# Layer 1's values by seven products, as a fourth stream beside queries, keys and outputs

## The chip, the cores and the metric

One Trainium2 chip, one core of it. The metric is device time in microseconds (us) of one execution. All data is 32-bit floating point. Engines: PE (TensorE, matmuls; its weight loads are listed as PEld), DVE (VectorE), ACT (ScalarE), POOL (GpSimd), SP (SyncE, which issues the transfers here).

## The reference

An image of 128 rows of 256 positions with 256 channels passes through two attention layers, each with a group normalization ahead of it and the input added behind it. Layer 0 is full attention inside each row (8 heads of 32) with a softmax, an added bias and a gate. Layer 1, where the change is, is attention inside each row too, in 4 heads of 64, where a position sees only positions at most 16 away:

```
qkv = x2 @ w_in.T + b_in                 # x2: 128 rows x (256 positions, 256 channels)
q, k, v = split(qkv)
scores = q k^T / 8, kept where |i - j| <= 16
out = softmax(scores) v
y = out @ w_out.T + b_out                # then x + y
```

## The kernel before, in words

Layer 1 handles two rows (a pair, number `i`) at a time; 64 pairs, of which the main loop runs over 63 (`i` = 0 to 62). A pair's normalized input `1xn` is [128 channels, 4, 256 positions], the 4 being (row, channel half).

A projection of a pair is a product of a 2x2 block weight with a 2x2 block input (two channel halves by two rows). The scheme used, with seven block products in place of eight (class `Seven`; `Summed` in layer 1), needs four sums of weight quarters (`Quarters`, made once, during layer 0) and four sums of input quarters (`1ts`, `row_sums`, on POOL: one 128x512 and two 128x256 subtractions). A stream's product `n` is written to one half of a PSUM bank; some products accumulate onto what is there, after ACT or DVE has taken the previous sum (`take`, L685 to L708). `in_turn` issues the streams in lockstep: product 2 of every stream, then product 1 of every stream, and so on in the order 2, 1, 5, 6, 7, 4, 3. While one stream's sum is taken, PE works for the others. There are three streams: `q` and `k` of pair `i + 1` and the output projection `o` of pair `i - 2`.

The values `v` of a pair do not go that way. `values` (L1380) computes them plainly, per row: 16 matmuls of 128x64 tokens with 128 output channels, eight block products in all. The result is stored by tokens: partition = position within a block of 64, with one half of the partitions for heads 0 and 1 (`half` 0) and the other for heads 2 and 3. One ACT copy per row (L1389) takes it.

One turn of the main loop issues, in this order (the order is written out by hand for all five engines, `manual_schedule`; nothing is reordered):

- `scores` of the two rows of pair `i` (L1409), ACT's exponentials (L1417), POOL's mask product `1p` (L1419) and sum `1zp` (L1426);
- `finish(i - 3)`: DVE transposes (L1562) and four stores of 128 KB (L1572) on SP's queue;
- `attend(i - 1)`: weights times values into `1av` (L1450; two PSUM banks, of which there is only one set, `bufs=1`), sums of weights `1zs` (L1462);
- `sums` (L1473, L1474) and three partial reciprocals `1rz` on DVE (`inverse`, L1487), the first at once, the other two inside the stretch after products 1 and 5;
- `stretch(i + 1, i - 2)`: the 21 products of the three streams, with `by_transfer(i - 1)` after product 5: `1rz` is written to `rz_far` (L1495, two small transfers) and read back, spread over partitions, as `1near` (L1499, two of 256 KB), on SP's queue;
- `normal(i + 2)`: the next input load `yg` (L796, 512 KB, SP's queue), four ACT activations into `1xn` (L1333), POOL's `1ts`;
- `divide(i - 1)`: two DVE products `1at` = `1av` x `1near` (L1519), which free `1av` for the next `attend`; then POOL's `row_sums` into `1att`;
- `bounds(i - 1)` (a DVE reduction L1528 and an ACT pass L1530 for a later check);
- `values` of the two rows of pair `i + 1`.

PSUM: `1av` and `1zs` have their own banks; scores, streams and values rotate through four banks of one ring (`proj_bank`).

Of the kernel before, what the change touches and what calls it, by code (L numbers as in the profile page):

```python
# [15 lines left out]
P = 128  # L16
# [23 lines left out]
def conv_preact_kernel(  # L40
# [536 lines left out]
    def row_sums(t, x, engine):  # L577

        engine.tensor_tensor(t[:, 0::2], x[:, 2:4], x[:, 0::2], ALU.subtract)  # L579
        engine.tensor_tensor(t[:, 1], x[:, 3], t[:, 0], ALU.subtract)  # L580
        engine.tensor_tensor(t[:, 3], x[:, 1], t[:, 1], ALU.subtract)
# [151 lines left out]
                    next(amid, lambda: None)()  # L733
                yield

    def in_turn(sevens, amid=lambda n: None, between=iter(())):


        for p in sevens:
            p.open()  # L740

            p.product(2, p.ps[:, 1, :], first=True)
            p.take(2)
        next(between, None)
        for n in (1, 5, 6, 7, 4, 3):
            for p in sevens:
                p.product(n)
                p.take(n)
            if n in (1, 5):
                amid(n)  # L750
            next(between, None)
        for _ in between:
            pass

    def one_by_one(w, at, name, done, width):

# [19 lines left out]
    with ExitStack() as both:  # L776
# [1 line left out]

        stats1 = st1.tile([P, 2, S // 2 + 2, 6], F32, name="stats1")
        most1 = Most(st1, stats1, 4, 1)  # L780
        quarters1 = {w: Quarters(st1, w_in_t, n * C, f"1{w}") for n, w in enumerate("qk")}
        quarters1["o"] = Quarters(st1, w_out_t, 0, "1o")
        ygs, pools = {}, {}
        rz_far = dram.tile([2, 2, 4, R], F32, name="rz_far")
# [3 lines left out]
        def load1(g):  # L788
            if g * XG < S and g not in ygs:

                if g % 7 < 2:
                    yg = big.tile([P, XG * (R // B), C // A], F32, tag="xg", name=f"yg{g}")
                    yg = yg.rearrange("p n c -> p (n c)").rearrange("p (s h q) -> p s h q", h=2, q=R)
                else:
                    yg = pools["yg"].tile([P, XG, 2, R], F32, tag="yg", name=f"yg{g}", bufs=5)
                nc.sync.dma_start(out=yg, in_=rows(x1, g * XG, XG))  # L796
                ygs[g] = yg
# [493 lines left out]
        with ExitStack() as lay:  # L1291
# [27 lines left out]

            shift1 = att.tile([P, 2], F32, name="shift1", bufs=1)  # L1320

            def normal(i, by_scalar):

                if 2 * i >= S:
                    return
                load1(i + 1)
                xns[i] = row.tile([P, 4, R], F32, tag="xn", name=f"1xn{i}", bufs=2)
                for r in range(2):
                    for half in (1, 0):
                        x, y = xns[i][:, 2 * r + half, :], ygs[i][:, r, half, :]  # L1330
                        col = slice(half, half + 1)
                        if by_scalar:
                            nc.scalar.activation(x, y, AF.Identity, bias=shift1[:, col], scale=rstd1[:, col])  # L1333
                        else:
                            nc.vector.tensor_scalar(
                                x, y, mean1[:, col], rstd1[:, col], op0=ALU.subtract, op1=ALU.mult
                            )
                tss[i] = row.tile([P, 4, R], F32, tag="ts", name=f"1ts{i}", bufs=2)
                row_sums(tss[i], xns[i], nc.gpsimd)

            def project(s):

# [18 lines left out]
                    st[2 * i + r].update({w: p.to[:, 2 * r : 2 * r + 2, :] for w, p in zip("qk", streams)})  # L1361
                return streams

            def stretch(i, j, amid=lambda n: None, between=iter(())):

                streams = projections(i)
                if j >= 0:
                    outputs[j] = Summed(row, quarters1["o"], ats[j], ats_t[j], f"1o{j}", "out", bias=bo_v, y=ygs[j])
                    streams.append(outputs[j])
                in_turn(streams, amid, between)  # L1370

            def values(s):
                if s >= S:
                    return
                i, r = divmod(s, 2)
                ps = proj_bank(f"p1v{s}").rearrange("p a (b c) -> p (a b) c", c=P)
                for b in range(NB):
                    for kt in range(2):
                        for half in range(2):
                            nc.tensor.matmul(  # L1380
                                ps[KB * half : KB * (half + 1), b, :],
                                lhsT=xns[i][:, 2 * r + kt, KB * b : KB * (b + 1)],
                                rhs=w_in_t[:, kt, 2 * C + P * half : 2 * C + P * (half + 1)],
                                start=(kt == 0), stop=(kt == 1),
                            )
                    if b < NB - 1:
                        yield
                v = row.tile([P, NB, P], F32, tag="v", name=f"1v{s}")
                nc.scalar.copy(v, ps)  # L1389
                st[s]["v"] = v  # L1390
                yield

            def all_values(rows):

                for s in rows:
                    yield from values(s)

            def scores(s, engine=nc.gpsimd):
                q, k = st[s]["q"], st[s]["k"]
# [29 lines left out]
            def attend(i):  # L1429

                if i < 0:
                    return

                if i < S // 2 - 1:
                    av = ps_av.tile([P, 2, 2, R], F32, tag="av", name=f"1av{i}", bufs=1)
                    av = [av[:, half] for half in range(2)]
                else:
                    av = [proj_bank(f"1av{i}_{half}") for half in range(2)]
                zs = ps_av.tile([P, 2, 2, R], F32, tag="zs", name=f"1zs{i}", bufs=1)
                zps = []  # L1440
                for r in range(2):
                    (p, zp), v = hd.pop(2 * i + r), st[2 * i + r]["v"]
                    zps.append(zp)
                    for b in range(NB):
                        for half in range(2):
                            for j in range(2):
                                keys, cols = slice(KB * half, KB * (half + 1)), slice(D1 * j, D1 * (j + 1))
                                q0, p0 = QLO[b], R * (b % 2) + QLO[b]

                                nc.tensor.matmul(  # L1450
                                    av[half][cols, r, q0 + QIN[b].start : q0 + QIN[b].stop],
                                    lhsT=v[keys, b, cols],
                                    rhs=p[keys, j, p0 + QIN[b].start : p0 + QIN[b].stop],
                                    start=(r == 0 and b == 0), stop=(b == NB - 1),
                                    skip_group_check=True,
                                )

                for r in range(2):
                    for half in range(2):
                        for j in range(2):  # L1460
                            keys = slice(KB * half, KB * (half + 1))
                            nc.tensor.matmul(  # L1462
                                zs[strip(2 * j + r), half, 0, :], lhsT=place[keys, :], rhs=zps[r][keys, j, :],
                                start=True, stop=True,
                            )
                hd["av", i] = (av, zs)
# [119 lines left out]
            with tc.manual_schedule(engines={  # L1586
# [9 lines left out]
                for i in range(last):  # L1596
                    s = 2 * i
                    scores(s)
                    scores(s + 1)
                    if i == 0:  # L1600
                        for _ in all_values(range(2)):
                            pass
                        normal(i + 2, True)
                        for _ in all_values(range(2, 4)):
                            pass
                        continue
                    finish(i - 3)
                    attend(i - 1)
                    sums(i - 1)
                    inverse(i - 1, 0)  # L1610

                    def amid(n):
                        inverse(i - 1, 1 if n == 1 else 2)
                        if n == 5:
                            by_transfer(i - 1)

                    stretch(i + 1, i - 2, amid, all_values(range(s + 2, s + 4)) if i == 1 else iter(()))
                    normal(i + 2, True)
                    divide(i - 1)
                    if 0 <= i - 1 < last - 2:  # L1620
                        ats_t[i - 1] = row.tile([P, 4, R], F32, tag="att", name=f"1att{i - 1}", bufs=2)
                        row_sums(ats_t[i - 1], ats[i - 1], nc.gpsimd)
                    bounds(i - 1)
                    if i > 1:
                        for _ in all_values(range(s + 2, s + 4)):
                            pass

                def all_of(s):
                    for _ in project(s):
# [6 lines left out]
                        store(s)  # L1636

                scores(S - 2)
                finish(last - 3)
                scores(S - 1, nc.vector)  # L1640
                attend(last - 1)
# [229 lines left out]
```

## Time and profile before

| | |
|---|---|
| time, median of 3 runs | 3087.22 us (3086.99 to 3087.53) |
| profiled execution: its time, its span | 3088.84 us, 3086.7 us |
| mean granted PE clock | 0.993 |
| from 2100 to 2300 us (layer 1): PE busy | 199.12 of 200 us |
| same stretch: PEld, DVE, ACT, POOL busy | 150.82, 131.57, 108.36, 139.44 us |
| same stretch: share of the DMA engines, rate | 0.43, 101 GB/s |
| layer 1: first product to end of the span | 2025.5 to 3086.7 us |

The span is what the profiler saw between the first and the last instruction; the execution's own time is 2.1 us longer. "Busy" is the time in which an engine had an instruction running; a matmul's row overlaps the next one's, so a duration in its row is longer than the distance between two starts. The chain of work that ended last lists pieces in the order in which each released the next; for PE its pieces are distances, and can be summed. "Idle before" with a releaser tells what an engine waited for. Offsets in the text are in us.

### The profile page before, as it was taken

To read this page: it belongs to the slowest core of one execution; us is meant where nothing else is said; L and a number is where in the kernel's file an instruction comes from. 1 tells how busy PE (TensorE), PEld (TensorE's weight loads), DVE (VectorE), ACT (ScalarE), POOL (GpSimd) and SP (SyncE) were. 2 spreads that over 40 slices of the span, in tenths; PEclk is the share of its full clock that TensorE was granted. 3 is DMA by queue.
4 is the path that set the end of the run, shared out by engine and by line. 5 is a ranking of instruction groups with operands and counts; after the bars stand their busy time and mean duration, and the time that the engine had idled before them with its cause. 6 is when DMAs were issued, how large, how long until landed. Compare 5 with 4: busy or idle time off the path is not lost.

```text
span 3086.7 us, 142499 instructions
## 1 busy us (share of the span) xinstructions
PE 3004.4 (97%) x62701; PEld 2062.4 (67%) x62701; DVE 2248.5 (73%) x4503; ACT 1913.6 (62%) x4327; POOL 1901.1 (62%) x1913
## 2 busy tenths in 40 slices
PE   7779999999999999999999999999999999999997
PEld 4546666666666666666666666677777777777775
DVE  4667787878787877787788778756666666666665
ACT  4656666667666766676667666655555555555553
POOL 3035666656665666566656565566677777777674
PEclk9989999999999999999999999999999999999999
DMA  9941222222222221222222222124444444444443
GB/s 379 424 135 45 62 65 62 50 64 65 62 50 63 65 61 49 65 64 60 52 65 62 61 52 65 58 64 102 102 96 100 105 99 99 97 104 99 98 98 71
DMA packets 385413, 280.84 MB, mean 91 GB/s; under 512 B 285104, under 2 KB 354192, under 8 KB 378640
## 3 DMA queue, kind: packets, MB, share of 16 engines
q1 hardware_dynamic: 383888, 269.27, 33.0%
q8 instruction: 494, 8.09, 1.1%
q0 software_dynamic: 752, 2.36, 0.2%
q14 instruction: 135, 1.11, 0.1%
q10 hardware_dynamic: 144, 0.00, 0.0%
HBM read 202.38 MB, written 69.17 MB: 88 GB/s over the span
## 4 chain that ended last, share of the span: by engine, by line
PE 91%; DMA 5%; DVE 2%; POOL 1%; issue 0%; ACT 0%; SPq 0%; DVEq 0%; POOLq 0%; ACTq 0%
PE sim L840 9%; PE av L872 7%; PE p1v L1380 7%; PE p1q L587 6%; PE pbv L936 6%; PE po L587 6%; PE p1k L587 6%; PE p1o L587 6%; PE pq L587 6%; PE pv L587 6%; PE pk L587 5%; PE pg L587 5%; PE zs L885 4%; PE 1sim L1409 3%; DMA pr<-in_L_conv_pair_repr_dram 3%; PE 1av L1450 3%
## 5 line engine op out<-in xcount | busy, mean ns | idle before, releaser
L853 ACT ACTIVATE ex<-sim 128x512 f32<-128x512 f32 x1024 | 555.2, 606 | 253.3 <-PE sim L840 253.3
L862 DVE TENSOR_TENSOR both<-ex 128x512 f32<-128x512 f32 x508 | 445.5, 896 | 65.7 <-ACT ex L853 65.4
L631 POOL TENSOR_TENSOR v<-v,midv 128x512 f32<-128x512 f32 x64 | 82.1, 1283 | 453.9 <-ACT v L625 453.9
L840 PE MATMUL sim<-q,k 32*64 32x256 f32 x8192 | 289.3, 388 | 1.3 <-ACT ex L853 1.3
L965 DVE RECIPROCAL rz<-zs 128x256 f32<-128x256 f32 x128 | 224.9, 1757 | 67.8 <-PE zs L885 55.9
L872 PE MATMUL av<-ex,v 128*32 128x256 f32 x4096 | 244.7, 379 | 1.6 <-DVE at L1030 1.6
L1419 POOL TENSOR_TENSOR 1p<-1ex,seen 128x768 f32<-128x768 f32 x127 | 231.4, 1822 | 11.4 <-ACT 1ex L1417 11.4
L691 ACT ACTIVATE 1q<-p1q,bqk 128x256 f32<-128x256 f32 x192 | 90.8, 473 | 236.6 <-PE p1q L587 118.3
L1380 PE MATMUL p1v<-w_in_t,1xn 128*64 128x128 f32 x4096 | 237.3, 273 | 0.0
L1380 PEld LDWEIGHTS p1v<-w_in_t,1xn 128*64 128x64 f32 x4096 | 232.1, 137 | 6.1
L579 POOL TENSOR_TENSOR 1ts<-1xn 128x512 f32<-128x512 f32 x64 | 81.4, 1271 | 249.1 <-ACT 1xn L1333 234.7
L840 PEld LDWEIGHTS sim<-q,k 32*64 32x64 f32 x8192 | 152.2, 131 | 113.6 <-issue 66.7
L631 POOL TENSOR_TENSOR q<-q,midq 128x512 f32<-128x512 f32 x64 | 82.0, 1281 | 197.1 <-ACT q L625 197.1
L872 PEld LDWEIGHTS av<-ex,v 128*32 128x32 f32 x4096 | 131.6, 110 | 79.1 <-DVE at L1030 2.1
L1519 DVE TENSOR_TENSOR 1at<-1av,1near 128x512 f32<-128x512 f32 x128 | 82.5, 686 | 126.5 <-DMA 1near<-rz_far 97.5
L1426 POOL TENSOR_TENSOR 1zp<-1p 128x512 f32<-128x512 f32 x127 | 162.3, 1278 | 10.0
L1389 ACT COPY 1v<-p1v 128x512 f32<-128x512 f32 x128 | 74.9, 586 | 122.0 <-PE p1v L1380 121.9
L343 DVE BATCH_NORM_STATS2 stats<-xs 128x6 f32<-128x128 f32 x512 | 100.3, 277 | 64.0 <-DMA xs<-in_x_dram 64.0
L885 PE MATMUL zs<-both,place 128*32 128x256 f32 x2032 | 137.5, 387 | 0.5 <-DVE both L862 0.5
L1029 DVE TENSOR_TENSOR av<-av,bv 128x512 f32<-128x512 f32 x125 | 87.4, 700 | 62.7 <-ACT bv L958 60.5
L1487 DVE RECIPROCAL 1rz<-1z 128x64 f32<-128x64 f32 (+1 forms) x192 | 129.8, 678 | 2.2
L1333 ACT ACTIVATE 1xn<-yg,shift,rstd 128x256 f32<-128x256 f32 x252 | 130.7, 591 | 0.6 <-DVE shift L1590 0.6
(355 smaller groups left out, 8308.8 us busy)
## 6 DMA issues: line engine op xcount, KB each, us to landing
pr<-in_L_conv_pair_repr_dram SPq DMA_DIRECT2D x32, 1024.0 KB
xs<-in_x_dram SPq DMA_DIRECT2D x16, 2048.0 KB
yg<-x SPq DMA_DIRECT2D x64, 512.0 KB
out_dram<-1o SPq DMA_DIRECT2D x256, 128.0 KB
xg<-in_x_dram SPq DMA_DIRECT2D x252, 128.0 KB
x<-o SPq DMA_DIRECT2D x63, 512.0 KB
near<-rz_far SPq DMA_DIRECT2D x500, 64.0 KB
1near<-rz_far SPq DMA_DIRECT2D x124, 256.0 KB
```

Source lines behind the costliest of these rows:

```text
L587: nc.tensor.matmul(out[cols], lhsT=lhsT[:, cols], rhs=rhs, **flags)
L631: nc.gpsimd.tensor_tensor(self.to[:, 2:4], self.to[:, 2:4], self.mid, ALU.add)
L840: nc.tensor.matmul(sims[j][KB * c : KB * (c + 1), kt, :], lhsT=k[p0 : p0 + D0, 2 * r + half, k0 : k0 + KB], rhs=q[p0 : p0 + D0, 2 * r + ha ...
L853: nc.scalar.activation(ex[:, j], sims[j], AF.Exp, scale=1.0 / math.sqrt(D0))
L862: engine.tensor_tensor(both[:, j : j + 2], ex[:, j : j + 2, 0, :], ex[:, j : j + 2, 1, :], ALU.add)
L872: nc.tensor.matmul(to[D0 * j : D0 * (j + 1), half, :], lhsT=v[:, 2 * r + half, c0 : c0 + D0], rhs=weights(4 * half + j, kt), start=(kt == ...
L885: nc.tensor.matmul(zs[strip(j), 0, :], lhsT=place0[:, half, :], rhs=both[:, j, :], start=(half == 0), stop=(half == 1),)
L936: nc.tensor.matmul(ps[strip(j), acc, half, :], lhsT=stationary[n][:, half, strip(j)], rhs=bias_of[n][:, 4 * half + j, :], start=(n <= 2 an ...
L965: nc.vector.reciprocal(rz, zs[:, 0, :])
L1380: nc.tensor.matmul(ps[KB * half : KB * (half + 1), b, :], lhsT=xns[i][:, 2 * r + kt, KB * b : KB * (b + 1)], rhs=w_in_t[:, kt, 2 * C + P * ...
L1419: engine.tensor_tensor(p.rearrange("p j (r c) -> p (j r) c", c=WROW)[:, :, 0 : 2 * WSTEP] .rearrange("p r (t c) -> p r t c", c=WSTEP)[:, : ...
L1426: engine.tensor_tensor(zp, p[:, :, 0:R], p[:, :, R : 2 * R], ALU.add)
```

## The change

The values become a fourth stream of the stretch (class `Tokens`), with weight sums of their own. It uses the same inputs `1xn` and `1ts` as `q` and `k`. Each of its seven products is four matmuls, with tokens as the stationary side, that put even blocks of 64 positions on one half of the partitions and odd blocks on the other. Its sums are taken by ACT copies, one DVE addition and two POOL additions. So half of the result lies on the wrong partitions for `attend`, and two transfers from SBUF to SBUF copy that half over (`other`). `attend` reads its stationary side from `own` or from `other`.

The order in the loop changes too: `normal(i + 2)` is cut in two shares, the first (with the load) after product 2, the second after product 6, each in the stretch; the second and third reciprocal and `by_transfer` come after product 1; `bounds` comes one turn later, ahead of `finish`; pairs 0 and 1 keep the plain `values`, with the same arithmetic as before.

```diff
+    class Tokens(Summed):
+        def product(self, n, two=None, first=False):
...
+            for b in range(R // KB):
+                nc.tensor.matmul(
+                    out[KB * (b % 2) : KB * (b % 2 + 1), P * (b // 2) : P * (b // 2 + 1)],
+                    lhsT=tokens[:, KB * b : KB * (b + 1)], rhs=self.weights.stationary(n),
+                    start=(n <= 2 and b < 2), stop=n in (2, 3, 4), skip_group_check=True,
+                )
+        def take(self, n):
+            to, ps = self.to, self.ps
+            if n == 2:
+                nc.scalar.copy(to[:, 0], ps[:, 1, :])
+            elif n == 1:
+                nc.scalar.copy(to[:, 2], ps[:, 0, :])
+                nc.gpsimd.tensor_tensor(to[:, 0], to[:, 0], to[:, 2], ALU.add)
+            elif n == 5:
+                nc.scalar.copy(to[:, 3], ps[:, 1, :])
+            elif n == 6:
+                nc.scalar.copy(self.mid, ps[:, 0, :])
+            elif n == 7:
+                nc.vector.tensor_tensor(to[:, 3], ps[:, 0, :], to[:, 3], ALU.add)
+            elif n == 4:
+                nc.scalar.copy(to[:, 1], ps[:, 0, :])
+            elif n == 3:
+                nc.scalar.copy(to[:, 2], ps[:, 1, :])
+                nc.gpsimd.tensor_tensor(to[:, 2], to[:, 2], self.mid, ALU.add)
...
+                tokens = Tokens(row, quarters1["v"], xns[i], tss[i], f"1v{i}", "v")
+                in_turn(streams + [tokens], amid)
+                other = row.tile([P, 2, R], F32, tag="vs", name=f"1vs{i}", bufs=2)
+                own = tokens.to.rearrange("p (r m) c -> p r m c", m=2)
+                for m in range(2):
+                    to, source = slice(KB * m, KB * (m + 1)), slice(KB * (1 - m), KB * (2 - m))
+                    nc.sync.dma_start(out=other[to], in_=own[source, :, m, :])
...
-                                    lhsT=v[keys, b, cols],
+                                    lhsT=vs[i](r, half, b)[:, cols],
...
+                    bounds(i - 2)
                     finish(i - 3)
                     attend(i - 1)
                     sums(i - 1)
                     inverse(i - 1, 0)
                     def amid(n):
-                        inverse(i - 1, 1 if n == 1 else 2)
-                        if n == 5:
+                        if n == 1:
+                            inverse(i - 1, 1)
+                            inverse(i - 1, 2)
                             by_transfer(i - 1)
-                    stretch(i + 1, i - 2, amid, all_values(range(s + 2, s + 4)) if i == 1 else iter(()))
-                    normal(i + 2, True)
+                        elif n in (2, 6):
+                            normal(i + 2, True, ((2, 6).index(n),))
+                    stretch(i + 1, i - 2, amid)
                     divide(i - 1)
...
-                    bounds(i - 1)
-                    if i > 1:
-                        for _ in all_values(range(s + 2, s + 4)):
-                            pass
```

More of the change, by code (lines that the diff above doesn't have):

```diff
@@ L734, in stream, with in_turn @@
                 yield
-    def in_turn(sevens, amid=lambda n: None, between=iter(())):
+    def in_turn(sevens, amid=lambda n: None):
         for p in sevens:
@@ L743, in in_turn @@
             p.take(2)
-        next(between, None)
+        amid(2)
         for n in (1, 5, 6, 7, 4, 3):
@@ L748, in in_turn, with __init__ @@
                 p.take(n)
[L749 to L752, printed above, removed]
-            pass
+            amid(n)
+    class Tokens(Summed):
+        def __init__(self, pool, weights, x, t, name, tag):
+            self.weights, self.x, self.t, self.name = weights, x, t, name
+            self.to = pool.tile([P, 4, R], F32, tag=tag, name=name, bufs=2)
+            self.mid = pool.tile([P, R], F32, tag=f"mid{tag}", name=f"mid{name}", bufs=1)
+        def product(self, n, two=None, first=False):
+            x, t = self.x, self.t
+            tokens = {1: x[:, 0], 2: x[:, 1], 3: x[:, 3], 4: t[:, 3], 5: t[:, 0], 6: t[:, 1], 7: t[:, 2]}[n]
+            out = self.ps[:, 1 if n in (2, 3, 5) else 0, :]
+            for b in range(R // KB):
[22 more added lines that the diff above has]
+                nc.gpsimd.tensor_tensor(to[:, 2], to[:, 2], self.mid, ALU.add)
     def one_by_one(w, at, name, done, width):
@@ L780, in conv_preact_kernel @@
         most1 = Most(st1, stats1, 4, 1)
-        quarters1 = {w: Quarters(st1, w_in_t, n * C, f"1{w}") for n, w in enumerate("qk")}
+        quarters1 = {w: Quarters(st1, w_in_t, n * C, f"1{w}") for n, w in enumerate("qkv")}
         quarters1["o"] = Quarters(st1, w_out_t, 0, "1o")
@@ L1320, in conv_preact_kernel, with normal @@
             shift1 = att.tile([P, 2], F32, name="shift1", bufs=1)
-            def normal(i, by_scalar):
+            def normal(i, by_scalar, shares=(0, 1)):
                 if 2 * i >= S:
                     return
-                load1(i + 1)
-                xns[i] = row.tile([P, 4, R], F32, tag="xn", name=f"1xn{i}", bufs=2)
-                for r in range(2):
+                for r in shares:
+                    if r == 0:
+                        load1(i + 1)
+                        xns[i] = row.tile([P, 4, R], F32, tag="xn", name=f"1xn{i}", bufs=2)
                     for half in (1, 0):
@@ L1337, in normal @@
                             )
-                tss[i] = row.tile([P, 4, R], F32, tag="ts", name=f"1ts{i}", bufs=2)
-                row_sums(tss[i], xns[i], nc.gpsimd)
+                    if r == 1:
+                        tss[i] = row.tile([P, 4, R], F32, tag="ts", name=f"1ts{i}", bufs=2)
+                        row_sums(tss[i], xns[i], nc.gpsimd)
             def project(s):
@@ L1362, in projections, with stretch @@
                 return streams
-            def stretch(i, j, amid=lambda n: None, between=iter(())):
+            vs = {}
+            def stretch(i, j, amid=lambda n: None):
                 streams = projections(i)
@@ L1369, in stretch @@
                     streams.append(outputs[j])
[L1370 to L1391, printed above, removed]
@@ L1393, in all_values @@
-            def all_values(rows):
-                for s in rows:
-                    yield from values(s)
+                tokens = Tokens(row, quarters1["v"], xns[i], tss[i], f"1v{i}", "v")
[5 more added lines that the diff above has]
+                    nc.sync.dma_start(out=other[to], in_=own[source, :, m, :])
@@ new lines, in part, with values @@
+                def part(r, half, b):
+                    what = own[:, r, half] if b % 2 == half else other[:, r]
+                    return what[KB * half : KB * (half + 1), P * (b // 2) : P * (b // 2 + 1)]
+                vs[i] = part
+            def values(i):
+                v = row.tile([P, 4, R], F32, tag="v", name=f"1v{i}", bufs=2)
+                v = v.rearrange("p (r t) (u c) -> p r (t u) c", r=2, c=P)
+                for r in range(2):
+                    ps = proj_bank(f"p1v{i}_{r}").rearrange("p a (b c) -> p (a b) c", c=P)
+                    for b in range(NB):
+                        for kt in range(2):
+                            for half in range(2):
+                                nc.tensor.matmul(
+                                    ps[KB * half : KB * (half + 1), b, :],
+                                    lhsT=xns[i][:, 2 * r + kt, KB * b : KB * (b + 1)],
+                                    rhs=w_in_t[:, kt, 2 * C + P * half : 2 * C + P * (half + 1)],
+                                    start=(kt == 0), stop=(kt == 1),
+                                )
+                    nc.scalar.copy(v[:, r], ps)
+                vs[i] = lambda r, half, b: v[KB * half : KB * (half + 1), r, b]
@@ L1441, in attend @@
                 for r in range(2):
-                    (p, zp), v = hd.pop(2 * i + r), st[2 * i + r]["v"]
+                    p, zp = hd.pop(2 * i + r)
                     zps.append(zp)
@@ L1600, in conv_preact_kernel @@
                     if i == 0:
-                        for _ in all_values(range(2)):
-                            pass
+                        values(0)
                         normal(i + 2, True)
-                        for _ in all_values(range(2, 4)):
-                            pass
+                        values(1)
                         continue
+                    bounds(i - 2)
                     finish(i - 3)
@@ L1622, in conv_preact_kernel @@
                         row_sums(ats_t[i - 1], ats[i - 1], nc.gpsimd)
-                    bounds(i - 1)
-                    if i > 1:
-                        for _ in all_values(range(s + 2, s + 4)):
-                            pass
                 def all_of(s):
@@ L1638, in conv_preact_kernel @@
                 scores(S - 2)
+                bounds(last - 2)
                 finish(last - 3)
```

## Prediction

> **What bounds the kernel now.** I read the page's busy times first, then the chain of work that ended last (all of it, then one turn of layer 1's loop), then the groups and the timeline around the two things that the change moves.
>
> ```profile
> PE 3004.4 (97%) x62701; PEld 2062.4 (67%) x62701; DVE 2248.5 (73%) x4503; ACT 1913.6 (62%) x4327; POOL 1901.1 (62%) x1913
> PE 91%; DMA 5%; DVE 2%; POOL 1%; issue 0%; ACT 0%; SPq 0%; DVEq 0%; POOLq 0%; ACTq 0%
> ```
>
> PE is busy nearly always and carries the chain, so matmul time removed counts in full, unless a wait appears in its place. One turn, from the chain between 2564.2 and 2581.1 (start, length, what):
>
> ```profile
> 2564.29 0.58 PE p1q L587 x4
> ...
> 2573.15 0.43 PE p1o L587 x4
> 2573.58 3.49 PE p1v L1380 x64
> 2577.07 1.48 PE 1sim L1409 x58
> ...
> 2578.64 1.21 PE 1av L1450 x63
> 2579.85 0.59 PE 1zs L1462 x16
> 2580.44 0.58 PE p1q L587 x4
> ```
>
> I count from the start S of the stretch (2564.29). 21 products take until S+9.29, the plain values until S+12.78, `1av` ends at S+15.56, and the next stretch starts at S+16.15, with no gap. Not every turn is like that. The `1z` additions (L1474) of consecutive turns lie 16.15 apart in most, and 16.2 to 17.1 in about a dozen of 60; the excess is 5 us in all. Three of these are explained by one late transfer, as in the chain between 2650 and 2664, where the work leaves PE:
>
> ```profile
> 2652.77 5.66 DMA 1near<-rz_far
> ...
> 2658.51 0.16 DVE 1at L1519
> ...
> 2659.81 0.14 issue
> 2659.95 1.44 PE 1av L1450 x64
> ```
>
> `1av` has one set of banks, so `attend` waits for the two divisions `1at` of the pair before. From the start of the first division to the end of `1av` (2659.95 + 1.44) it is 2.88 here. A turn that is not held up ends `1av` at S+15.56, so **a division that starts by S+12.68 costs nothing**. In the normal turn it starts at S+12.04, when `1near` lands; DVE itself was free at S+9.75:
>
> ```profile
> 2573.62 0.42 DVE L708 TENSOR_TENSOR 1o<-p1o,mid1o 128x256 f32<-128x256 f32 x1
> 2576.33 1.29 DVE L1519 TENSOR_TENSOR 1at<-1av,1near 128x512 f32<-128x512 f32 x2 [2.29 <-DMA 1near<-rz_far]
> ```
>
> **The change part by part.**
>
> *PE.* A pair's values are 64 rows of 128 columns in 3.49, or 54.5 ns each. Seven products of four matmuls are 56 such rows, with the same 64-column weights: 3.05. Removed: 0.44 per turn. Bounds: a product stands alone between products of 256 columns. If the pitch is the array's own (half of 0.43 for half the columns and twice the matmuls: 0.43 per product) it is 3.03; if each of 14 seams costs the 0.03 by which a few products in the chain are longer (0.46), it is 3.47 and nothing is gained. I take 3.05: weight loads in the plain values run as densely and hide. The stretch then lasts until S+12.34, and scores follow directly. 62 turns (i = 1 to 62): 27.1 us.
>
> *Takes.* ACT loses two copies of 128x512 (586 ns) and gets six of 128x256 (372 ns): +1.06, with 108 of 200 us busy. DVE gets one addition (425 ns), with 132 busy. POOL gets two additions of 128x256 (730 ns): +1.46 per turn, with 139 busy, so about 13 of 15.8. Do the takes hold PE? A stream's next product comes 4 x 0.43 = 1.74 after its last instead of 1.30, and a take is done 0.5 to 0.9 after its product. The two shares of `1xn` (1.04 each on ACT) fall between takes: after product 2 ACT is free at S+2.3 and next needed at S+3.6; after product 6 DVE has all takes of product 7. Cost nothing; without that cover a late take would add its lateness directly. On POOL `1ts` moves earlier, out of a wait:
>
> ```profile
> L579 POOL TENSOR_TENSOR 1ts<-1xn 128x512 f32<-128x512 f32 x58 | 73.7, 1271 | 223.1 <-ACT 1xn L1333 223.1
> L1389 ACT COPY 1v<-p1v 128x512 f32<-128x512 f32 x118 | 69.1, 586 | 113.6 <-PE p1v L1380 113.6
> ```
>
> (groups of 2100 to 3050.) That is 3.8 idle per turn, which holds the 1.46; `1att` is needed by the third round of the next stretch, some 3 after it is done. Nothing.
>
> *The moved half.* Two transfers of 128 KB wait on SP's queue for POOL's last addition (about 1.3 after the stretch), and behind them wait the stores, which are not ready before the transposes, 2.98 after the division begins. `1vs` is read a whole turn later; the nearest row, `1near`, takes 4.7 to 5.7 to land. No cost.
>
> *What the removed values had covered.* This is the step I weigh most. Before, 3.49 of plain values lay between `o`'s last product and the scores, and the division waited in that time. Now `v`'s last product alone (0.44) lies there. `o`'s last product ends at S+11.90; its take ends 0.46 later (2574.04 against 2573.58 above), so the division cannot begin before S+12.38, in DVE's own order. The limit moves with the stretch: `1av` would end at S+15.12, and with the division it ends at 12.38 + 2.88 = S+15.26. **A new wait of 0.14 in each turn**, 61 x 0.14 = 8.5 us. Were the takes to run ahead by that much it would be 0; I see no slack there, as DVE takes k and o back to back.
>
> *The transfers' order.* Both reciprocals now follow product 1: `o`'s take is done at S+3.64, and 0.94 + 0.54 later `rz_far` is issued, at about S+5.2 (before: S+5.09). But `yg` is now issued ahead of it, and the stores are later, since the division is: 12.38 + 2.98 is S-0.5 of the next turn, in place of S-1.1 (2579.31 against 2580.44):
>
> ```profile
> 2579.31 2.69 SPq L1572 DMA_DIRECT2D out_dram<-1o  x4
> 2585.53 1.10 SPq L1495 DMA_DIRECT2D rz_far<-1rz  x2
> 2587.16 1.12 SPq L1499 DMA_DIRECT2D 1near<-rz_far  x2
> 2588.38 0.53 SPq L796 DMA_DIRECT2D yg<-x  x1
> ```
>
> The Trainium skill (DMA: Bandwidth & Descriptors, "Queues, rings and completion order") says that each DMA engine consumes a queue's descriptors in ring order, and that a completion's semaphore write lands only after that engine's earlier writes. By this rule the tiny `rz_far` pays for `yg`: stores were on the engines until about 4.6 after their first issue, so until S+4.1; `yg`'s 512 KB at the 222 GB/s measured between 2588.2 and 2593.0 is 2.4 more, S+6.5, and `rz_far` lands at S+7.0 to 7.5. By its row alone (1.61 from issue, in the same chain) it is S+6.8. So `1near` starts 0.2 to 0.7 later by the rule. In return it no longer shares the engines with a `yg` behind it: before, it took 4.7 to 5.7 where its own 512 KB need 2.4. It lands at S+11.7 by the row, S+11.9 to 12.4 by the rule with nothing regained, and about S+11 to 11.5 with what I expect it to regain. All are within DVE's S+12.38; only the latest tenth would be late. I put its cost at nothing beyond the three late turns of before (1.1 us), and its bounds at -1 and +12 us (0.2 per turn).
>
> *The end.* There DVE also makes the last `1p`; it began 2.74 after the scores' start, and now comes behind division, reduction and transposes, 3.2 after: +0.5. POOL's four sums of weights in layer 0 (under 0.5 each) are beside PE's work: nothing.
>
> Sum: -27.1 + 8.5 + 0.5 = -18.1. From the profiled 3088.84 to 3070.8; from the median, 1.6 lower, **3069.2 us**.
>
> **Rivals.**
> - *No new wait* (the takes run ahead, or the divisions' second half is not what `attend` needs first): -27 us, 3060. For it: 0.14 is small against what I inferred. Against: DVE's order. Chance 0.22.
> - *The division waits on DVE*, as worked out: 3069. Chance 0.48.
> - *Seams or slightly late transfers*: 0.2 more per turn, +12: 3082, or up to 3090 with both. Chance 0.22, of which 0.08 below 3081.
> - *`1near` becomes the bound*: `yg` in front of `rz_far` delays it by 1.6 or more, so that it lands at S+13.3; then `1av` ends at S+16.2, 0.6 later than before, 62 times: 3125, slower. It decides from a landing at S+12.8. For it: the ring order. Against: the engines were idle (share 0.04) from 2583.5 to 2588.2, room that `yg` moves into. Chance 0.08.
>
> **How the numbers follow.** Within 0.2% (6.2 us, about what a measurement of this kernel can tell from no change) is 3081.0 to 3093.4. Faster: 0.22 + 0.48 + 0.08 = 0.78; same 0.14; slower 0.08. The range leaves out the slow rival and the worst of seams: 3057 to 3084; its lower end is full gain plus the late turns gone.
>
> **What would show it.** `1z` additions about 15.85 apart; `p1v` pieces of 0.43 to 0.44 in the chain; `1at` starting right behind `1o` (L708) with no wait for `1near`; `1av` held 0.1 to 0.2 by `1at`; POOL's wait for `1xn` shorter. I am wrong if `1at` waits for `1near`, if turns are 15.7 apart, or if PE waits inside the stretch for a take of `v`.

## The result and the profile after

The changed kernel takes 3056.9 us (median of 4 runs, 3054.35 to 3058.47) against 3087.1 us (4 runs). The ratio is 0.9903, with a 95% interval of 0.9886 to 0.992: 30 us faster. The forecast was 3069.2 us with a range from 3057 to 3084, so the direction was right, and the gain is 1.7 times the 18 us that the sum gave; the measured median lies 0.1 us below the range's lower end. What was measured is nearer to the forecast's rival of no new wait (3060 us). The profiled execution took 3056.63 us, with a span of 3054.9 us (before: 3086.7), 31.8 us shorter.

The page's busy times of the changed kernel:

```profile
PE 2975.4 (97%) x62205; PEld 2041.3 (67%) x62205; DVE 2266.9 (74%) x4565; ACT 1979.5 (65%) x4575; POOL 1993.2 (65%) x2041
```

PE has 496 matmul rows fewer, 8 for each of 62 turns, and still carries the chain (91%, as before). POOL, ACT and DVE all do more, and none of them became the bound. One turn, from the chain that ended last between 2564 and 2596 (start, length, what):

```profile
2564.09 0.58 PE p1q L587 x4
...
2575.92 0.44 PE p1v L764 x8
2576.36 1.48 PE 1sim L1452 x64
2577.84 1.34 PE 1av L1493 x64
2579.18 0.59 PE 1zs L1505 x16
2579.78 0.58 PE p1q L587 x4
```

The seven `v` products take 0.437 each on average, no more than the plain values' rate would give (3.49 / 8), so the seams between products of 256 and of 128 columns cost nothing. The turn, from one first `p1q` to the next, is 15.69 us, in place of 16.15. Where the 31.8 us came from, by the starts of the `1z` additions (L1474 before, L1517 after):

| part | before | after | difference |
|---|---|---|---|
| up to the first product of layer 1 on the chain | 2026.58 | 2026.42 | -0.16 |
| from there to the `1z` of the second turn with an `attend` | 35.37 | 34.61 | -0.76 |
| 60 turns, at 16.15 and 15.69 | 969.0 | 941.4 | -27.6 |
| excess: what longer turns have over that | 4.95 | 2.71 | -2.2 |
| the interval in which the loop ends | 18.36 | 17.81 | -0.55 |
| to the end | 32.50 | 32.08 | -0.42 |

The rows are rounded, so the differences add up to the 31.8 only within 0.1.

The division starts right behind the third take, as forecast. DVE's rows around it, in the same turn:

```profile
2575.61 0.42 DVE L708 TENSOR_TENSOR 1k<-p1k,mid1k 128x256 f32<-128x256 f32 x1
2575.97 0.42 DVE L708 TENSOR_TENSOR 1o<-p1o,mid1o 128x256 f32<-128x256 f32 x1
2576.31 1.28 DVE L1562 TENSOR_TENSOR 1at<-1av,1near 128x512 f32<-128x512 f32 x2
```

There is no bracket behind `1at`: here it does not wait for `1near`. But it starts at 2576.31, 0.08 ahead of the end of the row of `1o` (2576.39). From its start to the end of `1av` it is 2579.18 - 2576.31 = 2.87, the distance that the forecast had found (2.88) where the division does hold `1av`. In the kernel before, the row of `1k` likewise overlaps that of `1o`, which starts at 2573.62:

```profile
2573.26 0.42 DVE L708 TENSOR_TENSOR 1k<-p1k,mid1k 128x256 f32<-128x256 f32 x1
```

SP's queue in the turns after it:

```profile
2577.67 1.40 SPq L1414 DMA_DIRECT2D 1vs<-1v  x2
2579.28 3.24 SPq L1615 DMA_DIRECT2D out_dram<-1o  x4
2582.56 0.60 SPq L830 DMA_DIRECT2D yg<-x  x1
2584.72 1.47 SPq L1538 DMA_DIRECT2D rz_far<-1rz  x2
2586.61 1.26 SPq L1542 DMA_DIRECT2D 1near<-rz_far  x2
```

`1near` is issued 1.9 after `rz_far` here. Over 60 turns the median is 1.7 (before: 1.64, and never above 1.75); it is above 2.0 in 17 turns, and in three of these it is 2.7 to 3.2, and those three are late turns. So `yg` in front of `rz_far` does delay it, in part of the turns, and seldom by enough to matter.

What else changed is in the waits. Two pieces of a turn before, from the chain, are longer than the 0.43 of the others:

```profile
2567.03 0.48 PE p1q L587 x4
...
2569.24 0.46 PE p1o L587 x4
```

Some waits of PE's weight loads between 2100 and 3000 us, before: the longest, in which the load waited for nothing that the profile shows, and two that name a take (waiting instruction, releaser: us in total, times, longest):

```profile
PEld p1q L587 <- issue: 34.7, 103, 0.4
PEld p1q L587 <- ACT 1q L691: 25.8, 162, 0.2
PEld p1o L587 <- DVE 1o L685: 19.4, 111, 0.2
```

and all that are left for the changed kernel above 1.5 us:

```profile
PEld p1q L587 <- ACT 1same L1573: 20.2, 49, 0.4
PEld 1sim L1452 <- issue: 9.6, 56, 0.2
PEld p1q L587 <- issue: 3.2, 8, 0.4
PEld 1av L1493 <- POOL 1v L787: 1.9, 5, 0.8
```

The first comes about once a turn, with the stretch's first product, and names the ACT pass of `bounds`, not a take; the last belongs to late turns. With three streams a product's weight load waited for the take of its stream's last sum in nearly every round; with four, no such wait is among those left. Most of these waits of 0.2 did not hold PE's products up: only the pieces of 0.48 and 0.46 are longer.

### The profile page after: what moved, and what is told of

The parts are those of the page before. It is cut to its first block, busy times and chain, and to the rows that moved or that the text cites. A ratio compares the mean times of both kernels' runs of the same rounds, so it can differ in the third digit from the quotient of the medians.

```text
span 3054.9 us, 142260 instructions
## 1 busy us (share of the span) xinstructions
PE 2975.4 (97%) x62205; PEld 2041.3 (67%) x62205; DVE 2266.9 (74%) x4565; ACT 1979.5 (65%) x4575; POOL 1993.2 (65%) x2041
## 4 chain that ended last, share of the span: by engine, by line
PE 91%; DMA 5%; DVE 2%; POOL 1%; issue 0%; ACT 0%; SPq 0%; DVEq 0%; POOLq 0%; ACTq 0%
PE sim L874 9%; PE av L906 7%; PE po L587 6%; PE p1q L587 6%; PE pbv L970 6%; PE p1k L587 6%; PE p1v L764 6%; PE p1o L587 6%; PE pv L587 6%; PE pq L587 6%; PE pk L587 5%; PE pg L587 5%; PE zs L919 4%; PE 1sim L1452 3%; DMA pr<-in_L_conv_pair_repr_dram 3%; PE 1av L1493 3%
## 5 line engine op out<-in xcount | busy, mean ns | idle before, releaser
L1368 ACT ACTIVATE 1xn<-yg,shift,rstd 128x256 f32<-128x256 f32 x252 | 137.6, 597 | 0.6 <-DVE shift L1633 0.6
L685 DVE SCALAR_TENSOR_TENSOR 1o<-p1o,bo_v,yg 128x256 f32<-128x256 f32 x183 | 88.5, 484 | 51.7 <-PE p1o L587 49.5
L1530 DVE RECIPROCAL 1rz<-1z 128x64 f32<-128x64 f32 (+1 forms) x192 | 121.8, 663 | 2.2
L950 POOL TENSOR_TENSOR vt<-v 128x256 f32<-128x256 f32 x126 | 122.3, 970 | 0.0
L1460 ACT ACTIVATE 1ex<-1sim 128x384 f32<-128x384 f32 x256 | 105.2, 497 | 25.7 <-PE 1sim L1452 25.5
L587 PE MATMUL pq<-ts,sums_q 128*32 128x256 f32 x1536 | 118.5, 380 | 1.9 <-POOL ts L579 1.9
```

The costliest lines, as they stand in the source:

```text
L587: nc.tensor.matmul(out[cols], lhsT=lhsT[:, cols], rhs=rhs, **flags)
```

## Experiments

The theory after the result has three terms for a turn: the eighth product (-0.437), the takes' pacing of a round of three streams (-0.07), and a wait of `attend` for the division (+0.04 at most); besides, the loop's new order issues the load apart from the transfer, which may take late turns away. The rivals: the order brings the gain; the division does not bind; the moved half costs something.

### The order alone

Plain values stay, at the turn's end; everything else of the order is as in the changed kernel.

```diff
-                tokens = Tokens(row, quarters1["v"], xns[i], tss[i], f"1v{i}", "v")
-                in_turn(streams + [tokens], amid)
+                in_turn(streams, amid)
...
+                    values(i + 1)
```

> The new order of the loop (input in two shares, both reciprocals and the transfer after product 1, bounds a turn later) with the plain values, eight products, at the end of each turn; no fourth stream. Theory: the gain is the eighth product and a relief of the takes, so here the turn stays at 16.15 us, the chain still shows pieces of 0.48 and 0.46 in the stretch, and only the late turns can go: 3082 to 3087 us. Rival, the order itself brings the gain (transfer started away from the load): 3070 us or less, turns under 16.0.

Measured: 3095.77 us against 3087.93 us, ratio 1.0028 (1.0017 to 1.0038): slower than the kernel before. All turns are 16.33, with next to no late ones (excess 0.2). The expected time and turn missed; the rival, a gain from the order, is refuted. DVE's rows in one turn show where the 0.18 goes:

```profile
2570.72 0.43 DVE L698 TENSOR_TENSOR 1o<-p1o,1o 128x256 f32<-128x256 f32 x1
2571.06 1.35 DVE L1517 RECIPROCAL 1rz<-1z 128x128 f32<-128x128 f32 x2
2572.33 0.39 DVE L685 SCALAR_TENSOR_TENSOR 1o<-p1o,bo_v,yg 128x256 f32<-128x256 f32 x1
```

Two reciprocals in a row take 1.35, more than a round of 1.30, so the take of `o`'s product 5 is late; and the chain has PE's next `o` product held by it:

```profile
2572.87 0.64 PE p1o L587 x4
```

### The stream alone

```diff
-                        if n == 1:
-                            inverse(i - 1, 1)
-                            inverse(i - 1, 2)
-                            by_transfer(i - 1)
-                        elif n in (2, 6):
-                            normal(i + 2, True, ((2, 6).index(n),))
+                        if n in (1, 5):
+                            inverse(i - 1, 1 if n == 1 else 2)
+                        if n == 5:
+                            by_transfer(i - 1)
                     stretch(i + 1, i - 2, amid)
+                    normal(i + 2, True)
...
+                    bounds(i - 1)
```

> The fourth stream in, but the loop in the order of before: transfer after product 5, the whole input after the stretch, bounds in the same turn. Theory: the transfer is issued about 1 us later and the input's four activations stand ahead of the exponentials and of POOL's row sums, so that 1att or 1near is late: turns of 15.9 to 16.2, 3070 to 3085 us. Rival, the order does not matter: turns of 15.69, 3057 us.

Measured: 3069.6 us, ratio 0.9946 (0.9932 to 0.9959). Turns lie between 15.77 and 16.8, with a median of 15.88; time and median lie just under what was expected. The transfer is issued 5.9 to 6.0 after the stretch's start in the turns that were read, 1.0 later than in the changed kernel (2569.04 - 2564.09 = 4.95), as expected. Half of that lies behind the `1z` addition (4.88 from there in the median, against 4.41), where the third reciprocal now waits for product 5; the other half is that `1z` itself comes later. In the chain of one turn the work leaves PE for the transfer:

```profile
2578.03 1.64 DMA rz_far<-1rz
...
2580.28 4.40 DMA 1near<-rz_far
...
2584.80 0.13 DVE 1at L1562
...
2586.24 1.44 PE 1av L1493 x64
```

That `1z` is late comes from ACT's order: the input's four activations stand ahead of the exponentials, in a later turn (scores from 2616.58):

```profile
2616.95 2.08 ACT L1368 ACTIVATE 1xn<-yg,shift,rstd 128x256 f32<-128x256 f32 x4
...
2619.33 1.60 ACT L1460 ACTIVATE 1ex<-1sim 128x384 f32<-128x384 f32 x4
```

The exponentials start 2.75 behind the scores' start there, against 0.87 in the changed kernel.

So the stream in the old order gives 18 us of the 30, and the order alone loses 8: neither part is worth what it adds to the other. The round of four streams makes the room that the two reciprocals need; the new order, by the reciprocals and by the input's shares, starts the transfer early enough for a division that has no time left. How the loss divides between these two was not measured.

### The reciprocals apart again

As the order alone, but the third reciprocal and the transfer go back behind product 5.

```diff
-                        if n == 1:
-                            inverse(i - 1, 1)
-                            inverse(i - 1, 2)
-                            by_transfer(i - 1)
+                        if n in (1, 5):
+                            inverse(i - 1, 1 if n == 1 else 2)
+                            if n == 5:
+                                by_transfer(i - 1)
                         elif n in (2, 6):
```

> As the run with the order alone (plain values, three streams), but the third reciprocal and the transfer go back behind product 5. Theory: with three streams DVE has no room for two reciprocals in a row (1.35 us against a round of 1.30), so the output stream's take comes late and PE waits 0.18 a turn; with them apart the turn is 16.15 again and the time that of the kernel before, 3086 to 3089 us. Rival, another part of the order costs the 0.18 (the input's shares on ACT, bounds): 3094 us or more, turns of 16.3.

Measured: turns of 16.15, so it is the two reciprocals that cost the 0.18, and neither the input's shares nor `bounds`. The time is 3083.93 us, ratio 0.9988 (0.9981 to 0.9995), lower than expected: the late turns are gone (excess 0.31, before 4.95). What differs from the kernel before is that `yg` is issued in the stretch some 4 us ahead of the transfer and no longer right behind it, the input's shares, and `bounds` a turn later; that it is `yg` which takes the late turns away is likely, but was not shown alone.

### Half of the plain values between the rounds

As the order alone, but the first row's four blocks come one each after products 2, 1, 5 and 6.

```diff
+                        if n in (2, 1, 5, 6):
+                            next(between)      # 8 of the 64 matmul rows
```

> As the run with the order alone, but the first row's plain values are put between the rounds of products 2, 1, 5 and 6 (one quarter each), the second row's stay at the end; so eight products, no fourth stream, but four rounds of 1.74 us. Theory: the longer rounds alone take away the 0.18 and the 0.07 to 0.08 of takes' pacing that the kernel before has, so turns are 16.05 to 16.1 (about 3083 us), and the rest of the gain is the eighth product. Rival, the relief of the takes is most of the gain: turns under 15.9; rival, there is no relief: 16.15 or more.

Measured: 3079.13 us, ratio 0.9974 (0.9962 to 0.9985), turns of 16.08 to 16.09, excess 0.03. The chain of one turn, with only the pieces that are not 0.43 or 0.44, and without the cut ones at its edges:

```profile
2573.37 1.75 PE p1v L1420 x32
2575.12 1.49 PE 1sim L1447 x58
...
2576.69 1.21 PE 1av L1488 x63
2577.90 0.59 PE 1zs L1500 x16
```

No 0.48, 0.46 or 0.64 is left. The same matmuls as before, spread so that each of the first four rounds takes 1.74, take the 0.18 and 0.065 more away. This is the pacing by itself: 16.15 - 16.085 = 0.065. From 16.085 to 15.69 it is 0.395, which is the eighth product's 0.437 less 0.04. The 0.04 can be seen from the scores' start to the end of `1av`: 2577.90 - 2575.12 = 2.78 here, 2579.18 - 2576.36 = 2.82 in the changed kernel.

### The values' stream first in place of last

```diff
-                in_turn(streams + [tokens], amid)
+                in_turn([tokens] + streams, amid)
```

> The values' stream is issued first in each round in place of last; nothing else. Theory, the division's start in DVE's order sets the end of 1av: the last DVE take now ends one product (0.44 us) later against the scores, so turns are 0.40 to 0.44 longer, 16.1, and the time is about 3082 us. Rival, the division is not what limits: 3057 us.

Measured: 3081.72 us, ratio 0.9981 (0.9975 to 0.9988), turns of 16.12, 0.43 longer, as expected. The chain now passes through DVE at the end of the stretch:

```profile
2587.51 0.46 PE p1o L587 x4
2587.96 0.02 issue
2587.99 0.14 DVE 1o L708
2588.12 0.20 issue
2588.33 1.29 DVE 1at L1562 x2
2589.62 0.14 issue
2589.75 1.44 PE 1av L1493 x64
```

The turn grows by the whole product by which the take moved, so in the changed kernel the division has next to no slack: were there any, the turn would have grown by less. From the end of `o`'s product (2587.97) to the division it is 0.36. The place of the `v` stream, last in the round, is worth some 25 us.

### Without the two transfers

```diff
-                for m in range(2):
-                    nc.sync.dma_start(out=other[to], in_=own[source, :, m, :])
...
-                    what = own[:, r, half] if b % 2 == half else other[:, r]
+                    what = own[:, r, half] if b % 2 == half else own[:, r, 1 - half]
```

> The two transfers of the half on other partitions are left out, so attend reads wrong values for half of the blocks (all matmuls keep shape and number). Theory: they cost nothing, 3057 us within 1.5. Rival, their traffic makes the late turns that are left (2.75 us in all): 3054 us and no turn over 15.8.

This kernel leaves the moved half out, so half of the blocks use wrong values; its matmuls are the same.

Measured: 3058.79 us, ratio 0.991 (0.9895 to 0.9926), turns of 15.69, excess 4.45. The transfers cost nothing that can be measured, and their traffic is not what makes the late turns.

### The load behind the transfer, and in the middle

First, `load1(i + 3)` right behind `by_transfer(i - 1)`; then, in a second kernel, after product 4:

```diff
                             by_transfer(i - 1)
+                            load1(i + 3)           # first kernel
...
+                        elif n == 4:
+                            load1(i + 3)           # second kernel
```

> The changed kernel with the next input's load issued right behind the transfer of the reciprocals, as it was before the change, in place of ahead of it. Theory: the division's start is set by DVE in nearly all turns, with about 0.6 us of room behind the landing, so the turn stays at 15.69 and only turns in which 1near lands late come on top: 3057 to 3061 us. Rival, the load's place ahead of the transfer is what makes the gain: 1near lands later than S+12.2 in most turns, 3068 us or more.

Measured: 3061.07 us, ratio 0.9914 (0.9897 to 0.993), turns of 15.69 with late ones to 16.35. The rival is out: in the changed kernel the load's place is worth some us at most, as expected. The excess is 3.7.

> The changed kernel with the next input's load issued after product 4, some 3 us behind the transfer of the reciprocals, so that neither runs beside the other. Theory: turns of 15.69 as before, but the late turns whose 1near was late go; excess 0.3 to 1.5 us in place of 2.7, about 3055 us, a third of a per mille under the changed kernel on the same chip. Rival, the late turns have other causes: the same time within 1 us.

> The changed kernel itself, beside the run with the load after product 4 on the same chip: 3057 us, turns of 15.69 with an excess of some 2 to 4 us over all turns.

The second kernel does not move the load in time. SP's queue there:

```profile
2316.27 1.56 SPq L1543 DMA_DIRECT2D 1near<-rz_far  x2
2317.88 0.57 SPq L830 DMA_DIRECT2D yg<-x  x1
```

The load follows right behind the transfer, 7.3 after the `1z` addition in the median in both kernels: SP does not wait for product 4. So the load still runs beside `1near`, and the second kernel is in effect the first once more.

Measured: 3057.5 us with the load after product 4 (0.9905, 0.989 to 0.992) and 3059.72 us for the changed kernel on the same chip (0.9912, 0.9899 to 0.9926). The intervals overlap, so no winner is told, and the excess of 0.3 to 1.5 us that was expected did not come. In the trace the division's waits for `1near` all but go (one of 0.5 us, against five of 2.5 in all), but others stand in their place. Waits of PE's weight loads at `1av` with the load after product 4, between 2100 and 3000 us:

```profile
PEld 1av L1494 <- issue: 2.1, 5, 0.8
```

In these PE waits for nothing that the profile shows. The excess was 6.2 us there and 3.7 us in the first kernel with the load at the same place; it was 4.6 us in the repeat of the changed kernel, where its first profile had 2.7. So this part of the time varies from profile to profile, and is not settled.

### The sums of weights ahead of the products

`1zs` before `1av` in `attend`, the same matmuls.

> The changed kernel with attend's sums of weights (1zs) issued ahead of its products (1av); same work. The division gets 0.59 us more before 1av needs it, and the sums, reciprocals and transfer start earlier. Theory, the wait of 0.04 us and most late turns come from the division: turns of 15.65, excess under 1.5 us, 3052 to 3055 us. Rival, what is left is PE's own (matmul order and fetch): 3057 us or, if the changed order of tile shapes on PE costs, more.

Measured: 3056.63 us, ratio 0.9896 (0.988 to 0.9913), the same as the changed kernel's; the expected 3052 to 3055 us and turns of 15.65 did not come. Most turns are 15.72, no shorter. One of them:

```profile
2483.59 1.48 PE 1sim L1452 x64
2485.07 0.59 PE 1zs L1489 x16
2485.67 1.37 PE 1av L1501 x64
2487.04 0.58 PE p1q L587 x4
```

The division begins at 2483.73, that is 3.31 ahead of the end of `1av`, where 2.87 would do; so it does not hold `1av` here. Still the three groups take 3.45, against 3.42 in the changed kernel. So freeing the division is worth nothing here; either the 0.04 is not a wait for it, or PE loses as much by the other order. The two were not told apart.

## Why the prediction was right in direction and short in size

- **The eighth product**: right. 0.44 per turn forecast, 0.437 measured, seams at nothing.
- **Takes, POOL, ACT**: right in that none holds PE now. What the step missed is that takes *did* hold PE before: it took the 21 products as 9.29 and kept that time, 0.48 and 0.46 pieces included. Those were the takes' pacing, a term that the sum did not have. It is 0.065 per turn by itself (half of the values between the rounds), 4 us in all.
- **The moved half**: right, it costs nothing (run without the transfers).
- **What the removed values had covered**: the mechanism was right and the term was mis-sized. The forecast let the division begin 0.46 after the end of `o`'s last product, at the end of the take's row (its sum has S+12.38, where 11.90 + 0.46 is 12.36), and got a wait of 0.14. It begins 0.36 to 0.39 after it. On DVE the division starts ahead of the end of the last take's row; the rows `1k` and `1o` of the kernel before already had starts 0.36 apart with lengths of 0.42. The wait is at most 0.04. That is 0.1 per turn, 6 us. That the division is what comes next to holding PE is shown by the stream put first: one product later, and the whole 0.43 comes back. Turns 15.7 apart were the forecast's own sign that this term is wrong, and they are 15.69 apart.
- **The transfers' order**: the rule on ring order gave 0.2 to 0.7 of delay, the row's own time none. Measured, `1near` is issued 1.71 after `rz_far` in the median against 1.64, in the repeat of the changed kernel 1.89; it is above 2.0 in 17 and 26 turns of 60, and 2.7 or more in 3 and 6, which are late turns. With the load behind the transfer (before, and in both kernels with the load moved) it is never above 1.75. So the delay is there in part of the turns, as the rule has it, and DVE's order leaves room for all but a few. That `1near` regains time without `yg` behind it fits: in the three late turns it takes 3.9 to 4.0 in the chain, against the 4.7 to 5.7 of before. Its cost was put at nothing beyond the late turns of before; their excess was 4.95 before, and 2.71 and 4.6 in the two profiles of the changed kernel, so that they got fewer is not settled.
- **The end**: +0.5 forecast. The loop's last interval is 0.55 shorter, 0.46 of which is a turn's gain, so the 0.5 did not come; from there on it is 0.42 shorter, which was not looked into.
- Together: 0.065 + 0.1 per turn over 62 turns is 10 us; the late turns (2.2), the end (1.0) and the first turn (0.5) make up the other 4 of the 13.7 us by which the profiled gain exceeds the sum. The range's lower end stood for the full gain with the late turns gone; that the result lies there comes from other terms, and is in part luck.
- The two halves of the change were costed one by one, as if they added. They don't: -18 and +8 alone, -30 together.

## What to carry to other kernels

A stream added to a lockstep round lengthens the round, and so gives every other stream's takes more time; look for pieces of the chain that are longer than their neighbours, and for weight loads that wait for takes, before you call a stretch dense. When work that covered a latency is removed, find the instruction that has to start next and take its earliest start from the distance between starts of neighbouring rows, not from their ends. And try the parts of a change one by one before judging either: an order that loses in the old round can be what the new one needs.

## What the runs showed of the hardware that was not expected

- On DVE two additions of 0.42 that read PSUM started 0.36 apart, and a division started 0.08 ahead of the end of the row before it.
- 512 KB loaded ahead of two transfers of 4 KB on the same queue delayed the transfer that waits for these, the more often the shorter the distance between the issues. Without a load ahead the next issue came at most 1.75 after the small transfers. It was above 1.8 in 0 to 3 turns of 60 with the load 4.0 to 4.3 us ahead (the three kernels with plain values), in 13 with 3.2 (without the two transfers), and in 27 and 36 with 2.5 (the changed kernel and its repeat), there by more than 1 us in 3 and 6.
- PE paused at `1av` up to 0.8 us for nothing that the profile shows: between 2100 and 3000 us its weight loads did so 7 times in the kernel before, 2 and 5 times in the two kernels with the load behind the transfer, once in each profile of the changed kernel, and never with plain values and the load early. What causes it stays open.
